# A cross-attention and mixture-of-experts block: where weight reloads and stores stand on a queue, a running sum's engine, the order of background steps, and the ring of gathered rows

## The chip, the core and the metric

The kernel runs on one core of a Trainium2 chip, as one program. The time is in microseconds of the device (us), the median of several runs. One further execution was taken with the hardware profiler; all rows shown come from that one. TensorE (PE) multiplies matrices and PEld is its loading of weights; VectorE (DVE), ScalarE (ACT) and GpSimd (POOL) compute elementwise, and SyncE (SP) and POOL also issue DMA transfers. L12 in a row is line 12 of the kernel before.

## The reference

Two layers on four sequences of 512 tokens with 512 features. First a cross-attention whose probabilities come from a second input and mix the normalized rows, then a block with causal attention (16 heads of 128) and 16 experts, of which each token takes 6, beside a shared expert. Cut to what is computed:

```python
query = features @ Wq.T + bq
key = features @ Wk.T + bk
x = x + softmax(query @ key.T) applied to layernorm(x)

h = rmsnorm(layernorm(x), ln1_w)
q, k, v = h @ wq, h @ wk, h @ wv          # 16 heads of 128
a = softmax(causal(q @ k.T / sqrt(128)))
x1 = layernorm(x) + (a @ v) @ wo
t = rmsnorm(x1, ln2_w)
probs = softmax(t @ gate_w.T)
topv, topi = top_k(probs, 6); topv = topv / sum(topv)
routed = sum over the 6 experts e of topv * down_e(silu(gate_e(t)) * up_e(t))   # inner width 352
shared = sd(silu(sg(t)) * su(t))                                                # inner width 704
out = x + x1 + routed + shared
```

All values are float32 at the interface.

## The kernel before, in words

Every large product is made in three half-precision products: each operand is split into a high and a low f16 part, and `mm3` (L83, L86, L87) issues high by high, high by low and low by high into one bank. `split` makes the two parts, the high one on ACT (L73), the low one on DVE (L74).

**The stages.** `xattn(b)` is a generator: it normalizes batch b's rows, makes the cross-attention, stores the sum to `x_d` and leaves the transposed rows `hT[b]`. `step(b, n)` runs n of its pieces. Batch 0 is run to the end first, batch 1 begins before the heads, and the rest runs in the background of the loop over heads. That loop walks 64 heads (4 batches x 16) in the order of `path`, two heads to a group. For head n it issues `queries` (wqk, one product for query and key), for the first of a group `values` (wv), then `project` of a finished group (wo), `scores` of head n and `attend` of head n - 1 (LAG is 1). When a batch's groups are all projected, `route1`, `route2` and `route3` compute the router, the running place of each token in its expert's list, and the slots. Last in an iteration stand pieces of side work: the residual sums, the `scatter` of routed rows into `xs_d` (96 indirect DMAs on POOL, L467, one per tile of 128 tokens and rank), staging of the shared expert's weights, `pad_rows`, and `step`.

**Weights of the heads.** They are fetched by `fetch` (L406). The first time, a weight is loaded as f32 to a staging tile (L423, on POOL but for wqk1, which SP loads), split into a tile of f16 parts, and that tile is stored to a scratch in DRAM (L429). Later batches reload the f16 tile from there (L414, 40 reloads of 512 KB on POOL's queue). `partner` lets two batches that follow each other in `path` share one fetch. The pools `wp` (wqk) and `wg` (wv, wo) have two buffers for each tag.

**After the heads** come the shared expert of batches 0, 1 and 2 (`gate_up`, `shared_down`), and the 16 experts, ranked by their number of rows. `expert` runs in two halves: `gate_up_rows` makes the inner activation (hf, L1072, is the product of the gate and up branches on DVE, and hT_e, L1058 and L1059, its two f16 parts on ACT and DVE), `down_rows` the output rows yt (L1103 on ACT), which SP stores to `y_d`. Each expert's weights come by SP.

**The gathers.** Beside the last six experts and the last shared expert, the routed rows are gathered back. `gather` (L1169) is an indirect DMA on POOL of 128 rows of 512 f32 (256 KB) into a place of a ring, and `add` (L1178) on DVE multiplies such a tile with the router's weights and adds it to the batch's sum; the adds are held in program order. `lookahead(new, w, keep)` sets the ring: `w` rows share one tile, and `keep` gathers stay ahead of the adds. Before, the tile has three rows and takes turns in the two buffers of tag `hs` in pool `st2`, and four are kept ahead. `tick` spreads the gathers over an expert's steps. At the end of the experts `gather_all(0)` adds all that is left; the last shared expert then uses a ring of three tiles of three rows in pool `xin`, seven kept ahead.

**What sets the order.** The code does not fix it alone: the framework's scheduler places instructions by its own estimate of times and fixes the order on each engine. `pin` holds a few instructions in program order, `after(a, b)` adds an order between two instructions of one queue, without a semaphore. `pace` is a tiny copy on POOL that stands behind the scatters before it and waits for a given value, so that later scatters do not run ahead.

Of the kernel before, what the change touches and what calls it, by code (L numbers as in the profile page):

```python
# [9 lines left out]
F16 = mybir.dt.float16  # L10
F32 = mybir.dt.float32
# [6 lines left out]
P = 128  # L18
# [6 lines left out]
G = 8  # L25
# [14 lines left out]
CW = CAP - CUT  # L40
HB = 64
ON = 60
ROWS = E * T + 1

WS = 256.0
# [10 lines left out]
def xattn_moe_block_kernel(ctx: ExitStack, tc: tile.TileContext, x, xT, ctxT, wqkx, bqk, ln1, ln2,  # L56
# [345 lines left out]
        for j in range(0, 6 * D, 1024):  # L402
            pieces.append((sdw[:, :, j:j + 1024], sd[:, j:j + 1024]))

    held, partner, seen = {}, {}, set()

    def fetch(b, g, pool, tag, n, src, scr, nm):
        if held.get(nm, (None,))[0] == (b, g):
            return held.pop(nm)[1]
        w = pool.tile([P, 2, n], F16, tag=tag, name=f"{nm}_{b}")  # L410
        if (b, g) in partner:
            held[nm] = partner[b, g], w
        if nm in seen:
            nc.gpsimd.dma_start(w.rearrange("p a n -> p (a n)"), scr)  # L414
            return w
        seen.add(nm)
        first = nm in early_st
        if first:
            st_ = early_st[nm]
        else:  # L420
            st_ = stg.tile([P, 1024], F32, tag="st", name=f"{nm}_st")
            q = nc.sync if nm == "wqk1" else nc.gpsimd
            ins = q.dma_start(st_[:, :n], src)  # L423
            if nm == "wqk1":
                after(ins, zz["hT", 0])
        for j, ins in enumerate(split(w[:, 0], w[:, 1], st_[:, :n], WS)):
            if first:
                after(ins, zz["nb"] if j else zz["calm"][0])
        ins = (nc.sync if nm == "wqk0" else nc.gpsimd).dma_start(scr, w.rearrange("p a n -> p (a n)"))  # L429
        if nm != "wqk0":  # L430
            zz["pad"] = ins
        if nm == "wqk0":
            after(ins, zz["ptp", 0])
        return w

    pieces = []

# [17 lines left out]

    def pace(src):
        ins = nc.gpsimd.tensor_copy(mark, src)
        if "rrs" in zz:
            after(ins, zz["rrs"])
        for s in scats:  # L460
            after(ins, s)
        scats[:] = [ins]
# [69 lines left out]
    def route2(b):  # L532
        lg = bank("s", f"lg{b}")
        for t in range(NT):
            tl = slice(t * P, (t + 1) * P)
            n = 0
            for c in range(C):
                for a in range(2):
                    for e in range(2):
                        ins = nc.tensor.matmul(lg[:, t * E:(t + 1) * E], h2T[b][:, a * C + c, tl], gtp[:, e, c, :],  # L540
                                               start=n == 0, stop=n == 15)
                        if b == B - 1 and n == 0:
                            after(ins, zz["gu"])
                        n += 1

        bs = slice(b * NT, (b + 1) * NT)
        lgv = lg[:, :NT * E].rearrange("p (t e) -> p t e", e=E)
        mx = rp.tile([P, NT], F32, name="gmx", bufs=1)
        nc.vector.tensor_reduce(mx, lgv, AX.X, ALU.max)
        pr = rp.tile([P, NT, E], F32, name="gpr", bufs=1)  # L550
        nc.vector.tensor_tensor(pr, lgv, mx.unsqueeze(2).to_broadcast([P, NT, E]), ALU.subtract)
        zz["exp"] = nc.scalar.activation(pr, pr, AF.Exp, scale=PSC)
        sm = rp.tile([P, NT], F32, name="gsm", bufs=1)
        nc.vector.tensor_reduce(sm, pr, AX.X, ALU.add)
        rc = rp.tile([P, NT], F32, name="grc", bufs=1)
        nc.vector.reciprocal(rc, sm)
        nc.vector.tensor_tensor(pr, pr, rc.unsqueeze(2).to_broadcast([P, NT, E]), ALU.mult)
        v8 = rp.tile([P, NT, 8], F32, name="v8", bufs=1)
        i8 = rp.tile([P, NT, 8], U32, name="i8", bufs=1)
        for t in range(NT):  # L560
            nc.vector.max(v8[:, t, :], pr[:, t, :])
            nc.vector.max_index(i8[:, t, :], v8[:, t, :], pr[:, t, :])
        sv = rp.tile([P, NT], F32, name="gsv", bufs=1)
        nc.vector.tensor_reduce(sv, v8[:, :, :K], AX.X, ALU.add)
        rv = rp.tile([P, NT], F32, name="grv", bufs=1)
        nc.vector.reciprocal(rv, sv)
        ix = rp.tile([P, NT, K], F32, name="ix", bufs=1)
        nc.vector.tensor_copy(ix, i8[:, :, :K])
        oh = rp.tile([P, NT * K, E], F32, name="oh", bufs=1)
        nc.vector.tensor_tensor(  # L570
            oh, ix.rearrange("p t k -> p (t k)").unsqueeze(2).to_broadcast([P, NT * K, E]),
            ioe.unsqueeze(1).to_broadcast([P, NT * K, E]), ALU.is_equal)
        mf = rp.tile([P, NT, E], F32, name="mf", bufs=1)
        nc.vector.tensor_reduce(mf, oh.rearrange("p (t k) e -> p t e k", k=K), AX.X, ALU.add)
        mm = rp.tile([P, NT, E], F16, name="mm", bufs=1)
        nc.vector.tensor_copy(mm, mf)
        cs = mf
        for sft in (1, 2, 4, 8):
            nx = rp.tile([P, NT, E], F32, name="rcs", bufs=2)
            nc.vector.tensor_copy(nx[:, :, :sft], cs[:, :, :sft])  # L580
            nc.gpsimd.tensor_tensor(nx[:, :, sft:], cs[:, :, sft:], cs[:, :, :E - sft], ALU.add)
            cs = nx
        nc.gpsimd.tensor_tensor(cs, cs, mf, ALU.mult)
        nc.gpsimd.tensor_tensor(pr, pr, rv.unsqueeze(2).to_broadcast([P, NT, E]), ALU.mult)
        zz[b] = oh, mm, cs, pr
# [36 lines left out]

    def values(b, g):
        hb = hT[b]
        wvt = fetch(b, g, wg, "wv", C * GW, wv[g], wv_d[g], f"wv{g}").rearrange("p a (c d) -> p a c d", c=C)
        vt = vts[b, g] = vp.tile([P, NT, 2, GW], F16, tag="vt", name="vt")
        for t2 in range(0, NT, 2):
            if t2:
                yield
            ps = bank("a", f"v{b}_{g}_{t2}").rearrange("p (t d) -> p t d", t=2)  # L630
            for t in range(t2, t2 + 2):
                tl = slice(t * P, (t + 1) * P)
                mm3(ps[:, t - t2], [(hb[:, c, tl], hb[:, C + c, tl], wvt[:, 0, c], wvt[:, 1, c])
                                    for c in range(C)])
            split(vt[:, t2:t2 + 2, 0], vt[:, t2:t2 + 2, 1], ps, VS * PSC)

    def queries(b, h):
        hb = hT[b]
        wt = fetch(b, h // HG, wp, "wqk", 1024, wqk[h], wqk_d[h], f"wqk{h}").rearrange("p l (a c d) -> p l a c d", a=2, c=C)
        qk = qks[b, h] = []  # L640
        pss = [bank("a", f"qk{b}_{h}_{a}") for a in range(2)]
        w = S // 2 if b == h == 0 else S
        for j in range(0, S, w):
            if j:
                yield
            for a in range(2):
                mm3(pss[a][:, j:j + w], [(wt[:, 0, a, c], wt[:, 1, a, c], hb[:, c, j:j + w], hb[:, C + c, j:j + w])
                                         for c in range(C)])
        for a, ps in enumerate(pss):
            t = hq.tile([P, 2, S], F16, tag=f"qk{a}", name=f"qkt{a}")  # L650
            split(t[:, 0], t[:, 1], ps, PSC * (4.0 / math.sqrt(HD) if a == 0 else 0.25))
            qk.append(t)
# [42 lines left out]
    def project(b, g):  # L695
# [1 line left out]
            x2s[b] = x2p.tile([P, NT, D], F32, tag="x2", name="x2")  # L697
            nc.gpsimd.dma_start(x2s[b], hid_d[b])
        ao, x2 = aos[b, g], x2s[b]
        wot = fetch(b, g, wg, "wo", HG * D, wo[g], wo_d[g], f"wo{g}").rearrange("p a (c d) -> p a c d", c=HG)  # L700
        for t in range(NT):
            tl = slice(t * P, (t + 1) * P)
            ps = bank("w", f"wo{b}_{g}_{t}")
# [76 lines left out]
    for n in range(NH + LAG + 1):  # L780
        if n < NH:
# [13 lines left out]
            for p in parts:  # L795
                for _ in p:
                    pass
        m = n - LAG
        if n == NH:
            last_residual(B - 1)  # L800
# [17 lines left out]
        if 0 <= m < NH:  # L818
            b, h = heads[m]
            attend(b, h)  # L820
            if h % HG == HG - 1:
                ready.append((b, h // HG))
        if n in agenda and n < NH:
            b = agenda[n]
            if n + 1 in agenda:
# [6 lines left out]
        if scat and n < NH:  # L832
            scatter(-(-len(scat) // (min(x for x in ends if x > n) - n + (4 if n > NH - 3 else 0))))
        shared_weights()
        if H // 2 <= n < H // 2 + E:
            pad_rows(n - H // 2)
        if n < 6:
            step(1, 2)
        else:
            for _, j in zip(range(2 - n % 2), bring):  # L840
                step(j)
# [3 lines left out]
    shared_down(0, hs0)  # L845
    cctx.close()
    st2 = ctx.enter_context(tc.tile_pool(name="st2", bufs=2, side="right", reuse_waits="tile"))

    def up(b):
        return gate_up(b, lambda: st2.tile([P, 6 * S], F16, name="hs"), lambda: st2.tile([P, S], F32, name="sgt"))  # L850

    def drip(n, src):
        if scat:
# [340 lines left out]
        for _ in range(-(-len(todo) // left)):  # L1194
            gather()

    lookahead(lambda: st2.tile([P, 3, D], F32, tag="hs", name="yg"), 3, 4)
    ring["steps"] = 1
    for e in range(E):
        wd = nxt  # L1200
        for h, _ in enumerate(expert(wd, e)):
# [4 lines left out]
            if e + 1 < E:  # L1206
# [2 lines left out]
                rows_in(e + 1, h)  # L1209
                if h == 0:  # L1210
                    nxt = ranked_weights(e + 1)
    gather_all(0)
    lookahead(lambda: xin.tile([P, 3, D], F32, tag="xT", name="yg"), 3, 7)
    flush()
    want(K - 1, yrc, cws, y_d)
# [78 lines left out]
```

## Time and profile before

| | |
|---|---|
| runs, us | 1768.77, 1769.27, 1786.13 |
| median, us | 1769.27 |
| the profiled execution, us | 1762.41 |
| its span, us | 1760.7 |
| PE busy | 1708.6 us (97%) |
| DVE busy | 1116.2 us (63%) |
| ACT busy | 829.3 us (47%) |
| POOL busy | 485.1 us (28%) |
| routed rows gathered (L1169) | 96, 109.9 us of POOL |
| routed rows scattered (L467) | 96, 98.7 us of POOL |

The span is what lies between the first and the last instruction in the profile; the execution has 1.7 us around it. The median is 6.9 us above the profiled execution. Busy time of an engine sums its instructions, so an engine at 97% has 52 us in which it does nothing. In the rows of a timeline the columns are the start, the duration, the engine, the line and operation, output and input with shapes, and in brackets the idle time before the instruction and what ended it.

How the span is shared out, in 40 slices of 44 us, each digit the busy share in tenths:

```profile
PE   7899999999998999999999999999999999999998
DVE  6787877787785676776667647544434344356755
POOL 5524212240255242121113454300000000034654
DMA  7787867575687787556547653755554546589866
```

PE is full but for the first slice. POOL is idle while the first ten experts run, and busy again when the gathers begin; there the DMA engines are at their fullest too.

### The profile page before, as it was taken

To read this page: it belongs to the slowest core of one execution; us is meant where nothing else is said; L and a number is where in the kernel's file an instruction comes from. 1 tells how busy PE (TensorE), PEld (TensorE's weight loads), DVE (VectorE), ACT (ScalarE), POOL (GpSimd) and SP (SyncE) were. 2 spreads that over 40 slices of the span, in tenths; PEclk is the share of its full clock that TensorE was granted. 3 is DMA by queue.
4 is the path that set the end of the run, shared out by engine and by line. 5 is a ranking of instruction groups with operands and counts; after the bars stand their busy time and mean duration, and the time that the engine had idled before them with its cause. 6 is when DMAs were issued, how large, how long until landed. Compare 5 with 4: busy or idle time off the path is not lost. (4 is left out here: it accounts for less than half of the span.)

```text
span 1760.7 us, 27659 instructions
## 1 busy us (share of the span) xinstructions
PE 1708.6 (97%) x9919; PEld 932.9 (53%) x9919; DVE 1116.2 (63%) x2766; ACT 829.3 (47%) x1711; POOL 485.1 (28%) x614
## 2 busy tenths in 40 slices
PE   7899999999998999999999999999999999999998
PEld 3555556565654555556555544455555555555553
DVE  6787877787785676776667647544434344356755
ACT  4565655565643545454445422344544445444431
POOL 5524212240255242121113454300000000034654
PEclk9999999999999999999999999999999999999999
DMA  7787867575687787556547653755554546589866
GB/s 246 181 205 184 225 150 192 122 196 118 138 183 187 163 177 179 120 120 118 111 104 132 140 155 128 247 173 148 150 173 137 154 143 163 154 228 254 221 198 213
DMA packets 392212, 296.24 MB, mean 168 GB/s; under 512 B 334880, under 2 KB 335136, under 8 KB 391296
## 3 DMA queue, kind: packets, MB, share of 16 engines
q1 hardware_dynamic: 353360, 159.87, 39.9%
q0 software_dynamic: 38704, 134.51, 25.5%
q8 instruction: 80, 1.31, 0.3%
q14 instruction: 68, 0.56, 0.1%
HBM read 124.81 MB, written 88.94 MB: 121 GB/s over the span
## 5 line engine op out<-in xcount | busy, mean ns | idle before, releaser
L1169 POOL DMA_INDIRECT yg<-y_d,yrc x96 | 109.9, 1145 | 505.2 <-PE u L87 426.0
L673 ACT ACTIVATE pe<-pe,bnm 128x128 f32<-128x128 f32 (+3 forms) x256 | 142.5, 557 | 161.5 <-DVE bnm L671 161.3
L83 PE MATMUL qk<-hT,wqk 128*128 128x512 f16 (+1 forms) x520 | 196.4, 378 | 9.1 <-DMA wqk<-wqk_d 5.5
L86 PE MATMUL qk<-hT,wqk 128*128 128x512 f16 (+1 forms) x520 | 196.5, 378 | 0.0
L87 PE MATMUL qk<-hT,wqk 128*128 128x512 f16 (+1 forms) x520 | 196.3, 377 | 0.0
L74 DVE SCALAR_TENSOR_TENSOR pn<-pe,brc,pn 128x128 f16<-128x128 f32 (+3 forms) x256 | 148.1, 590 | 21.3 <-ACT pn L73 18.0
L671 DVE CUSTOM_DVE_ANT_0 pe<-sc,causal 128x128 f32<-128x128 f32 (+3 forms) x256 | 117.0, 485 | 66.9 <-PE sc L668 65.9
L73 ACT ACTIVATE pn<-pe,brc 128x128 f16<-128x128 f32 (+3 forms) x256 | 133.5, 553 | 34.1 <-ACT pe L673 17.8
L83 PE MATMUL v<-wv,hT 128*128 128x256 f16 x512 | 139.8, 273 | 0.9 <-DMA hT<-hh 0.9
L87 PE MATMUL v<-wv,hT 128*128 128x256 f16 x512 | 139.7, 273 | 0.0
L86 PE MATMUL v<-wv,hT 128*128 128x256 f16 x512 | 139.7, 273 | 0.0
L83 PE MATMUL g<-xT,wt 128*128 128x384 f16 (+2 forms) x384 | 127.3, 331 | 0.0
L86 PE MATMUL g<-xT,wt 128*128 128x384 f16 (+2 forms) x384 | 127.2, 331 | 0.0
L87 PE MATMUL g<-xT,wt 128*128 128x384 f16 (+2 forms) x384 | 127.2, 331 | 0.0
L1058 ACT ACTIVATE hT_e<-hf 128x384 f16<-128x384 f32 (+3 forms) x96 | 51.1, 532 | 133.6 <-DVE hf L1072 133.2
L83 PE MATMUL y<-dt,hT_e 128*128 128x512 f16 (+1 forms) x288 | 109.4, 380 | 0.0
L87 PE MATMUL y<-dt,hT_e 128*128 128x512 f16 (+1 forms) x288 | 108.9, 378 | 0.0
L86 PE MATMUL y<-dt,hT_e 128*128 128x512 f16 (+1 forms) x288 | 108.9, 378 | 0.0
L73 ACT ACTIVATE qkt<-qk 128x512 f16<-128x512 f32 x128 | 75.1, 587 | 70.7 <-PE qk L87 70.5
L705 DVE SCALAR_TENSOR_TENSOR x<-wo,x 128x512 f32<-128x512 f32 x128 | 87.2, 685 | 33.3 <-PE wo L87 32.9
L467 POOL DMA_INDIRECT xs_d<-h2p,slotu x96 | 98.7, 1028 | 28.3 <-issue 27.1
L74 DVE SCALAR_TENSOR_TENSOR qkt<-qk,qkt 128x512 f16<-128x512 f32 x128 | 87.5, 684 | 18.3 <-ACT qkt L73 15.2
(333 smaller groups left out, 4041.5 us busy)
## 6 DMA issues: line engine op xcount, KB each, us to landing
y_d<-yt SPq DMA_DIRECT2D x96, 256.0 KB, 2.8
est<-in_ew_dram SPq DMA_DIRECT2D x32, 704.0 KB, 6.2
est<-in_ed_dram SPq DMA_DIRECT2D x16, 768.0 KB, 4.7
wqk<-wqk_d POOLq DMA_DIRECT2D x20, 512.0 KB, 5.0
wqk_d<-wqk POOLq DMA_DIRECT2D x15, 512.0 KB, 4.0
wqk_st<-in_wqk_dram POOLq DMA_DIRECT2D x14, 512.0 KB, 6.4
xs_d<-causal POOLq DMA_DIRECT2D x16, 384.0 KB, 5.6
wv<-wv_d POOLq DMA_DIRECT2D x10, 512.0 KB, 5.7
```

What stands on the lines that cost most here:

```text
L73: return (nc.scalar.activation(hi, src, AF.Copy, scale=scale), nc.vector.scalar_tensor_tensor(lo, src, scale, hi, ALU.mult, ALU.subtract))
L74: nc.vector.scalar_tensor_tensor(lo, src, scale, hi, ALU.mult, ALU.subtract))
L83: ins = nc.tensor.matmul(o, lh, rh, start=start and j == 0, stop=False)
L86: nc.tensor.matmul(o, lh, rl, start=False, stop=False)
L87: ins = nc.tensor.matmul(o, ll, rh, start=False, stop=stop and j == n - 1)
L467: ins = nc.gpsimd.indirect_dma_start(out=xs_d, out_offset=bass.IndirectOffsetOnAxis(ap=slotu[:, tt, k:k + 1], axis=0), in_=h2ps[tt], in_of ...
L671: nc.vector.tensor_tensor_reduce(pe, ps[:, :w], causal[:, S - w:], -1.0, 3e38, ALU.add, ALU.min, nm)
L673: nc.scalar.activation(pe, pe, AF.Exp, bias=nm, scale=-1.0, accum_out=sm)
L705: nc.vector.scalar_tensor_tensor(x2[:, t, :], ps, 1.0 / (VS * WS), x2[:, t, :], ALU.mult, ALU.add)
L1058: nc.scalar.activation(hT[:R, ic, :w], hf, AF.Copy)
L1169: nc.gpsimd.indirect_dma_start(out=yg, out_offset=None, in_=src, in_offset=bass.IndirectOffsetOnAxis(ap=idx[:, tt, k:k + 1], axis=0))
```

## The change

Six edits.

1. `fetch` gets a flag `early`. With it, a reload is issued and the tile is kept in `soon` until its user asks for it. Heads n + 1's wqk and, where a group begins, wv are asked for right after the queries and values of head n; wo is asked for after `attend` of the group's last head. Weights that have not been staged yet are left to the old place.
2. Stores of staged weights to the scratch are collected in `unsaved`. The next staging load, once issued, is followed by all that wait, in an order on POOL's queue; what is left is issued at the ends of groups.
3. `pace`'s copy is also ordered behind the last reload.
4. The sixteen additions of the routing's running sum (four for each batch) run on DVE, which also makes the copies between them.
5. In the first heads the background of batch 1's cross-attention runs in steps of 3 for heads 1 to 5 (no piece at head 0) where it ran in steps of 2 from head 0.
6. The ring of gathered rows has seven tiles of one row, with five kept ahead, in a pool of its own, which takes the place of the two `hs` tiles. The last shared expert takes its `hs` tiles from the buffers of the experts' weights, so the ring stays open through it; the ring is not drained before the last expert's rows are stored.

```diff
-    held, partner, seen = {}, {}, set()
-
-    def fetch(b, g, pool, tag, n, src, scr, nm):
+    held, partner, seen, soon = {}, {}, set(), {}
+
+    def wqk_of(b, h, early=False):
+        return fetch(b, h // HG, wp, "wqk", 1024, wqk[h], wqk_d[h], f"wqk{h}", early)
+
+    def wv_of(b, g, early=False):
+        return fetch(b, g, wg, "wv", C * GW, wv[g], wv_d[g], f"wv{g}", early)
+
+    def wo_of(b, g, early=False):
+        return fetch(b, g, wg, "wo", HG * D, wo[g], wo_d[g], f"wo{g}", early)
+
+    def fetch(b, g, pool, tag, n, src, scr, nm, early=False):
+        if early and nm not in seen or soon.get(nm) and early:
+            return
         if held.get(nm, (None,))[0] == (b, g):
-            return held.pop(nm)[1]
-        w = pool.tile([P, 2, n], F16, tag=tag, name=f"{nm}_{b}")
+            return None if early else held.pop(nm)[1]
+        w = soon.pop(nm, None)
+        if w is None:
+            w = pool.tile([P, 2, n], F16, tag=tag, name=f"{nm}_{b}")
+            if nm in seen:
+                zz["load"] = nc.gpsimd.dma_start(w.rearrange("p a n -> p (a n)"), scr)
+        if early:
+            soon[nm] = w
+            return
         if (b, g) in partner:
             held[nm] = partner[b, g], w
         if nm in seen:
-            nc.gpsimd.dma_start(w.rearrange("p a n -> p (a n)"), scr)
             return w
         seen.add(nm)
         first = nm in early_st
@@ -423,15 +441,24 @@
             ins = q.dma_start(st_[:, :n], src)
             if nm == "wqk1":
                 after(ins, zz["hT", 0])
+            save(0, None if nm == "wqk1" else ins)
         for j, ins in enumerate(split(w[:, 0], w[:, 1], st_[:, :n], WS)):
             if first:
                 after(ins, zz["nb"] if j else zz["calm"][0])
-        ins = (nc.sync if nm == "wqk0" else nc.gpsimd).dma_start(scr, w.rearrange("p a n -> p (a n)"))
-        if nm != "wqk0":
-            zz["pad"] = ins
         if nm == "wqk0":
-            after(ins, zz["ptp", 0])
+            after(nc.sync.dma_start(scr, w.rearrange("p a n -> p (a n)")), zz["ptp", 0])
+        else:
+            unsaved.append((scr, w))
         return w
+
+    unsaved = []
+
+    def save(keep, behind=None):
+        while len(unsaved) > keep:
+            scr, w = unsaved.pop(0)
+            zz["pad"] = nc.gpsimd.dma_start(scr, w.rearrange("p a n -> p (a n)"))
+            if behind:
+                after(zz["pad"], behind)
...
     def pace(src):
         ins = nc.gpsimd.tensor_copy(mark, src)
-        if "rrs" in zz:
-            after(ins, zz["rrs"])
+        for k in ("rrs", "load"):
+            if k in zz:
+                after(ins, zz[k])
...
-            nc.gpsimd.tensor_tensor(nx[:, :, sft:], cs[:, :, sft:], cs[:, :, :E - sft], ALU.add)
+            nc.vector.tensor_tensor(nx[:, :, sft:], cs[:, :, sft:], cs[:, :, :E - sft], ALU.add)
...
+            if n + 1 < NH:
+                b, h = heads[n + 1]
+                wqk_of(b, h, True)
+                if h % HG == 0:
+                    wv_of(b, h // HG, True)
...
             if h % HG == HG - 1:
                 ready.append((b, h // HG))
+                wo_of(b, h // HG, True)
...
+        if n % HG == HG - 1:
+            save(1)
+        if n >= 3 * G:
+            save(0)
...
         if n < 6:
-            step(1, 2)
+            step(1, 3 * (n > 0))
...
+    hctx = ctx.enter_context(ExitStack())
+    hsp = hctx.enter_context(tc.tile_pool(name="hsp", bufs=2, side="right", reuse_waits="tile"))
 
     def up(b):
-        return gate_up(b, lambda: st2.tile([P, 6 * S], F16, name="hs"), lambda: st2.tile([P, S], F32, name="sgt"))
+        return gate_up(b, lambda: (hsp.tile([P, 6 * S], F16, name="hs") if b < B - 1 else
+                                   mw.tile([P, IP * 4], F32, tag="est", name="hs", bufs=3).bitcast(F16)),
+                       lambda: st2.tile([P, S], F32, name="sgt"))
...
-    lookahead(lambda: st2.tile([P, 3, D], F32, tag="hs", name="yg"), 3, 4)
+    hctx.close()
+    ring_p = ctx.enter_context(tc.tile_pool(name="ring", bufs=RING, side="right", reuse_waits="tile"))
+    lookahead(lambda: ring_p.tile([P, 1, D], F32, name="yg"), 1, RING - 2)
...
-    gather_all(0)
+    gather_all()
     lookahead(lambda: xin.tile([P, 3, D], F32, tag="xT", name="yg"), 3, 7)
```

The uses of `fetch` in `queries`, `values` and `project` become `wqk_of`, `wv_of` and `wo_of`; `RING` is 7.

More of the change, by code (lines that the diff above doesn't have):

```diff
@@ L42 @@
 ON = 60
+RING = 7
 ROWS = E * T + 1
@@ L624, in values @@
         hb = hT[b]
-        wvt = fetch(b, g, wg, "wv", C * GW, wv[g], wv_d[g], f"wv{g}").rearrange("p a (c d) -> p a c d", c=C)
+        wvt = wv_of(b, g).rearrange("p a (c d) -> p a c d", c=C)
         vt = vts[b, g] = vp.tile([P, NT, 2, GW], F16, tag="vt", name="vt")
@@ L638, in queries @@
         hb = hT[b]
-        wt = fetch(b, h // HG, wp, "wqk", 1024, wqk[h], wqk_d[h], f"wqk{h}").rearrange("p l (a c d) -> p l a c d", a=2, c=C)
+        wt = wqk_of(b, h).rearrange("p l (a c d) -> p l a c d", a=2, c=C)
         qk = qks[b, h] = []
@@ L699, in project @@
         ao, x2 = aos[b, g], x2s[b]
-        wot = fetch(b, g, wg, "wo", HG * D, wo[g], wo_d[g], f"wo{g}").rearrange("p a (c d) -> p a c d", c=HG)
+        wot = wo_of(b, g).rearrange("p a (c d) -> p a c d", c=HG)
         for t in range(NT):
```

## The prediction, before the change was run

> **What bounds the kernel now.** I read the page's engine totals first, then TensorE's waits, then those waits by stretch of the span, then the timeline around the longest ones. TensorE is busy 1708.6 of 1760.7 us (97%), so everything in this change plays for the 52.1 us in which it is not busy, plus what a long pause costs afterwards in clock. TensorE's waits (columns: total us, times, longest):
>
> ```profile
> PE av L83 <- DMA pt<-pn: 16.9, 10, 3.9
> PE xm L83 <- DMA ptp<-pn: 9.8, 2, 5.8
> PE qk L83 <- DMA wqk<-wqk_d: 5.5, 1, 5.5
> PE u L1081 <- DVE hf L1072: 3.9, 2, 2.1
> PE qk L83 <- DMA hT<-hh: 3.6, 2, 3.2
> ```
>
> The largest row, the flipped probabilities (pt), is touched by no edit. A weight reload is waited for once, the ranked experts' end twice. By stretch (length, then busy time and instructions of PE, PEld, DVE, ACT, POOL; PE clock; DMA share; GB/s):
>
> ```profile
> 88.00:540.00 452.00, 446.32 (x2742) 254.97 (x2740) 354.50 (x986) 254.94 (x570) 134.32 (x183) 1.00 0.72 172
> 540.00:1016.00 476.00, 458.45 (x2879) 263.85 (x2878) 323.32 (x938) 234.30 (x556) 136.88 (x207) 0.99 0.64 140
> 1016.00:1544.00 528.00, 527.98 (x2831) 269.34 (x2830) 241.10 (x476) 219.86 (x371) 58.45 (x81) 1.00 0.55 160
> 1544.00:1650.00 106.00, 102.08 (x573) 55.85 (x572) 66.41 (x101) 44.61 (x79) 48.76 (x43) 1.00 0.91 239
> ```
>
> Idle: 5.7 us in the first heads, 17.5 in the later ones, nothing in 1016-1544, 3.9 where gathers run beside experts, 17.2 before 88 us and about 8 after 1650. The timeline at the places that the edits touch:
>
> ```profile
> 76.60 0.58 PE L83 MATMUL xm<-ptp,lnp 128*128 128x512 f16 x1 [3.97 <-DMA ptp<-pn]
> 138.86 0.38 PE L83 MATMUL qk<-hT,wqk 128*128 128x512 f16 x1 [0.39 <-DMA hT<-hh]
> ...
> 538.93 0.96 POOL L467 DMA_INDIRECT xs_d<-h2p,slotu  x1 [0.30 <-issue]
> 539.89 0.60 POOL L414 DMA_DIRECT2D wqk<-wqk_d  x1
> 548.81 0.61 PE L83 MATMUL qk<-hT,wqk 128*128 128x512 f16 x1 [5.51 <-DMA wqk<-wqk_d]
> ...
> 1615.89 1.22 POOL L1169 DMA_INDIRECT yg<-y_d,yrc  x1 [4.15 <-DVE acc L1178]
> 1620.09 1.43 DVE L1178 SCALAR_TENSOR_TENSOR acc<-yg,cws,acc 128x512 f32<-128x512 f32 x2 [3.81 <-DMA yg<-y_d,yrc]
> 1621.57 0.60 ACT L1103 ACTIVATE yt<-y 128x512 f32<-128x512 f32 x1 [6.72 <-DMA y_d<-yt]
> 1626.41 0.32 PE L1081 MATMUL u<-xT,wb 128*128 128x384 f16 x1 [2.13 <-DVE hf L1072]
> ```
>
> The reload is issued 8.9 us before TensorE goes on and stands behind ten scatters of about 1.28 us each on POOL (525.7 to 539.9); TensorE came for it at 543.3.
>
> **Part 1, reloads ahead.** The change issues a reload at the end of the queries or values before. I compared the two programs' order on POOL: all 40 reloads stand where they stood, but for one (head 1's wqk ahead of wo, where TensorE waited for neither), and each waits for the same matmul to free its buffer. The framework's scheduler already issued them as early as the two buffers allow. The one that TensorE waits for is still behind the same ten scatters. Its buffer was free at about 534.9, when qk of the head before was done; only a place ahead of the last four scatters would gain. So the 5.5 us stay: 0. Bounds: a gain of 5.5 plus about 2.5 for 549-553, where the granted clock is 0.50 (8 in all), if the timing of these ten scatters slips behind it; a loss of a scatter step, 1.3.
>
> **Part 2, stores behind loads.** 31 stores of weights (0.56 us of issue each) move behind the next staging load on POOL, one or two places. Nothing is added. Store and load take the same queue; the next writer of the same weight buffer, two fetches later, waits longer. ACT's share of the splits already waits 26.1 us in 15 places for these stores, and behind it stand exponentials. Yet TensorE waits for no split weight at all, because the splits end before it comes for them (a head lasts 1016 / 64 = 15.9 us): that hides it, 0. Without that cover each of the 15 would cost TensorE its mean, 1.7 us. The added order of the mark behind the load is on one queue: no semaphore, 0.
>
> **Part 3, running sum.** POOL loses 12 x 269 ns + 4 x 294 = 4.4 us. DVE has no such row; the nearest, a 128x64 tensor-tensor, takes 0.19 to 0.22, so 16 x 0.2 = 3.2 us are added. The waits of DVE for POOL's sum (4.1 us in 3) go. The ten scatters start when the rank matmul is done (520.1) and DVE's rb (520.4), not on these. On no path of TensorE: 0, bounds -1.6 (the scatters' start moves by the longest of these waits) to +1.
>
> **Part 4, the next batch's cross-attention in steps of 3 for heads 1-4.** This does reorder TensorE: the first third differs from 72 us to 540, the rest is the same but for two or three rows. At 72.4 TensorE took the flip's matmul and waited 3.97 us; then some ten matmuls at half rate (0.427 against 0.2155 us apart, about 1.5-2 us lost). In the new order two score matmuls come first, waiting for DVE reads at 75.34 and 75.95: 2.98 + 0.3 us. Gain 4.0 - 3.3 = 0.7. Whether the half clock goes with it is weighed here. The Trainium skill ("TensorE: Matmul & The Clock Gate", section "HAM oscillation — how this bites in real kernels") has TensorE throttled by idle windows of about 3.4 us; by it 2.98 would escape, and the gain would be about 2.2. In this trace 3.23 us of idle at 51.3 already halved the rate, and 2.48 at 585 did not. 2.98 lies between, nearer to 3.23; the row decides, I take 0.7 and keep 2.2. hT of batch 1 is made a head earlier, which ends 138.86's wait: -0.4. What is late next: the exponentials and pt flips of heads 1-5 meet a denser cross-attention. Bounds: the first heads' 4.8 us of pt waits gone, or the later heads' density (12 us in 476) over 452: 11.4, 6.6 more. No row prefers either: 0.
>
> **Part 5, the gather ring.** Six rows as two tiles of three become seven single rows. Before, the first gather of a tile waits for an add issued just before it; now for one that stands two gathers back. POOL's 45.1 us of waiting for adds (16 times) mostly goes, but POOL binds nothing here. Two TensorE pauses end in this stretch. At 1645.26 (1.80 us) hf stood on DVE behind an add whose gather had waited 6.5 us for its tile: gone, -1.8. At 1626.41 (2.13) ACT's yt waited for a store of y_d, under a full DMA load (share 0.91): I take half, -1.0. No drain at the ring's end: adds move on, DVE is 66 of 106 us busy, 0.
>
> A rule that speaks against a gain is "DMA: Bandwidth & Descriptors", section "Anatomy of one DMA — SWDGE (gpsimd) path": about 2.0 us plus bytes over 436 GB/s, so 2.6 us for a gather of 256 KiB. By that, four adds of lookahead (4 x 0.745 = 3.0 us of DVE) cover every gather and the ring is worth nothing, and 548.81's load (512 KiB, 3.2 us) would have landed at 543.1, before TensorE came. The rows say otherwise:
>
> ```profile
> L1169 POOL DMA_INDIRECT yg<-y_d,yrc x96: 953/960/2612, 1551.4 to 1739.6; - x96
> DMA to landing us min/median/max: 3.3/4.7/10.6
> ```
>
> so the row is taken. By the rule the sum is -1.1, by the rows: -0.7 - 0.4 - 1.8 - 1.0 = -3.9.
>
> **Sum.** The profiled run took 1762.41 (span 1760.7 and 1.7 around it): 1762.4 - 3.9 = 1758.5. The median of the runs, 1769.27, is 6.9 above it; against that: 1765.4, so 1765.
>
> **Rivals.** *Faster by more than the sum.* The reload's stall and its half clock vanish (8), part 4 gives 2.2 and the early pt waits 4.8, the ring all 3.9, hT 0.4: 19.3, so 1750. For it: slots are free 5 us before that reload goes out. Against: POOL's order, which is fixed, puts the ten scatters ahead.
>
> *Slower, by the ring.* Five gathered rows now wait ahead of the adds and up to seven gathers fly, where DMA is at 0.91 already. A gather's packets then delay y_d's stores; yt waits for these (28.7 us in 9 waits of ACT after 1540), hT behind yt on ACT, and TensorE takes a pause as at 1626.41. Price: about 2 us for each of the ten half experts, 20 in all: 1789. It decides when the y_d stores regularly land over 7.6 us, as before that pause; their median is 3.6 after 1540. For it: two pauses of this form stand there already. Against: the number of rows moved is the same, and TensorE paused twice in 106 us.
>
> *The change does not do what it says.* The reloads come no earlier, the ring was never on the path, and the reordered heads trade one wait for another: 0 to +8, so 1769 to 1777.
>
> **How the numbers follow.** Forecast 0.54; no effect or a small loss 0.22; faster rival 0.10; slower rival 0.14. One per cent, about what a measurement of this kernel can tell, is 17.7 us: faster means under 1751.6, slower over 1787.0. Only the two rivals reach beyond: faster 0.10, same 0.76, slower 0.14. The range leaves out the faster rival's far half and most of the slower one: from 1752 (the reload's 8, the ring, 2.2, hT and half of the pt gain, 17) to 1780 (6.6 of pt, 1.3 of scatter, 3 more of ring).
>
> **What would show it.** Right: 5 to 6 us of wait for wqk<-wqk_d near 545 behind ten scatters; 2.9 us at the first scores near 75; no pause behind hf near 1640, POOL's waits for acc well under 45. Wrong: a wait list for pt far from 17 us; the reload issued well before TensorE needs it; y_d's stores landing over 7 us and new pauses at L1081. The forecast fails if the head stretch up to 540 moves by more than 7 us either way.

## The result, and the profile after

| | before | after |
|---|---|---|
| median, us | 1769.11 (21 runs) | 1787.38 (21 runs) |
| range, us | 1754.3 to 1786.13 | 1773.52 to 1798.73 |
| the profiled execution, us | 1762.41 | 1776.03 |
| its span, us; granted clock | 1760.7; 0.993 | 1774.2; 0.991 |

The ratio is 1.0114, with a 95% interval of 1.009 to 1.0137: the change costs some 20 us, where 4 us less were forecast, and the median lies 7 us above the range. The profiled execution is the second fastest of its 21 runs, so its 13.5 us of longer span show the loss too small. The run at the median, 1787.38, has a span of 1785.7 and a granted clock of 0.986 where the profiled one has 0.991; 0.014 x 1785.7 against 0.009 x 1774.2 is 25 against 16 us, so by this estimate up to 9 of the 11 us between the two spans lie in the clock. In rows of other kernels than the one before, the line numbers are those of that kernel.

TensorE's waits in the changed kernel (total us, times, longest):

```profile
PE av L84 <- DMA pt<-pn: 19.5, 11, 6.1
PE qk L84 <- DMA hT<-hh: 7.1, 2, 3.9
PE xm L84 <- DMA ptp<-pn: 6.0, 1, 6.0
PE u L1123 <- DVE hf L1114: 4.4, 2, 3.0
PE xixp L1020 <- DVE xixd L1018: 2.8, 1, 2.8
PE sc L695 <- DVE qkt L75: 2.7, 1, 2.7
PE qk L84 <- DMA wqk<-wqk_d: 2.5, 1, 2.5
```

The flip of the cross-attention's probabilities (ptp) is waited for 3.8 us less, the reload (wqk) 3.0 less. Against this stand the transposed rows hT with 3.5 more, pt with 2.6 more, and two new rows, xixp and qkt. The sums hide where it happens. By stretch (columns as before):

```profile
88.00:540.00 452.00, 433.55 (x2638) 245.90 (x2637) 344.72 (x957) 242.81 (x542) 125.95 (x168) 0.99 0.70 165
540.00:1016.00 476.00, 465.86 (x2942) 269.44 (x2940) 331.13 (x968) 239.67 (x569) 141.81 (x207) 0.99 0.64 143
1544.00:1650.00 106.00, 101.64 (x563) 55.19 (x562) 64.00 (x97) 45.03 (x79) 48.06 (x39) 0.98 0.94 231
```

TensorE is idle for 18.4 us in the first heads where it was for 5.7, for 10.1 in the later ones where it was for 17.5, and for 4.4 beside the gathers where it was for 3.9. The same product found in both traces, and how much later it starts after the change:

| product | before, us | after, us | lag, us |
|---|---|---|---|
| qk, the 193rd | 157.6 | 160.2 | 2.6 |
| qk, the 577th | 392.5 | 404.4 | 11.9 |
| qk, the 769th | 517.9 | 529.7 | 11.8 |
| qk, the 1057th | 699.1 | 702.9 | 3.8 |
| g, the first of the experts | 1134.0 | 1140.2 | 6.2 |
| g, the 1057th | 1656.3 | 1664.4 | 8.1 |
| the end | 1760.7 | 1774.2 | 13.5 |

The first heads lose 11.9 us, against the 7 that the prediction named as its point of failure; the waits for pt and the reload between 518 and 700 give 8 back in this execution, and the rest comes after 1000: xixp's 2.8 us near 1114, some 2 us more beside the gathers, and some 3 us in five pauses of the last shared expert, near 1735 to 1741, that wait for nothing that the profile shows. The cause of these was not tried. Two pauses stand at the start of the loss; the timeline of the changed kernel has

```profile
142.24 0.38 PE L84 MATMUL qk<-hT,wqk 128*128 128x512 f16 x1 [3.85 <-DMA hT<-hh]
180.77 0.61 PE L84 MATMUL av<-pt,vt 128*128 128x512 f16 x1 [6.11 <-DMA pt<-pn]
```

The first is the wait that the prediction saw vanish (0.39 us at 138.86 before). What happened around it is in the issues of two transfers: the last flip of batch 1's hT (a DMA transpose on SP's queue, DMA_TRANSPOSE) and the 1 MB load of batch 2's x. Before:

```profile
135.76 1.26 SPq L91 DMA_TRANSPOSE hT<-hh  x1
136.59 0.84 POOL L215 DMA_DIRECT2D xt<-in_x_dram  x1 [0.30 <-POOL x L354]
```

After, with the other transfers of POOL at this place:

```profile
127.88 0.54 POOL L459 DMA_DIRECT2D wo_d<-wo  x1
131.05 0.85 POOL L216 DMA_DIRECT2D xt<-in_x_dram  x1 [0.30 <-POOL x L355]
131.81 2.60 SPq L92 DMA_TRANSPOSE hT<-hh  x1
134.46 0.54 POOL L441 DMA_DIRECT2D wqk_st<-in_wqk_dram  x1 [2.56 <-DVE wo L75]
134.99 0.54 POOL L459 DMA_DIRECT2D wo_d<-wo  x1
```

Before, the flip goes out 0.83 us ahead of the load and is used 3.1 us later. After, it goes out 0.76 us behind the load and is used 10.4 us later.

### The profile page after: what moved, and what is told of

Its sections match the earlier page's. It is cut to its first block, busy times and chain, and to the rows that moved or that the text cites. A ratio compares the mean times of both kernels' runs of the same rounds, so it can differ in the third digit from the quotient of the medians.

```text
span 1774.2 us, 27650 instructions
## 1 busy us (share of the span) xinstructions
PE 1714.3 (97%) x9919; PEld 933.1 (53%) x9919; DVE 1120.1 (63%) x2782; ACT 827.9 (47%) x1711; POOL 492.4 (28%) x598
## 5 line engine op out<-in xcount | busy, mean ns | idle before, releaser
L1211 POOL DMA_INDIRECT yg<-y_d,yrc x96 | 118.0, 1229 | 505.0 <-DVE hf L1114 434.6
L495 POOL DMA_INDIRECT xs_d<-h2p,slotu x96 | 98.8, 1030 | 28.0 <-issue 26.8
```

The costliest lines, as they stand in the source:

```text
L495: ins = nc.gpsimd.indirect_dma_start(out=xs_d, out_offset=bass.IndirectOffsetOnAxis(ap=slotu[:, tt, k:k + 1], axis=0), in_=h2ps[tt], in_of ...
L1211: nc.gpsimd.indirect_dma_start(out=yg, out_offset=None, in_=src, in_offset=bass.IndirectOffsetOnAxis(ap=idx[:, tt, k:k + 1], axis=0))
```

## The experiments

Each ratio is against the kernel before on the same chip, with its 95% interval. The chips differ between the groups of runs, so across groups it is the ratios that are compared, not the times.

**The heads, the ring, the steps, the stores, each by itself** (e1 to e4). e1 has all edits but the running sum and the ring; e2 has the ring alone, the diff of which stands above.

```diff
+            step(1, 3 * (n > 0))                        # e3, alone
...
+            save(0, None if nm == "wqk1" else ins)      # e4, alone, with save at the group ends
```

> The kernel before with the edits to the heads alone: early reloads, stores behind loads, the mark behind the load, steps of 3; the running sum on POOL and the old ring. Theory A (the reordered first heads cost it: waits for hT near 142 and for pt near 181, with half a clock after each): 1.007 to 1.012 of before, +12 to +21 us, and a profile with waits of 3 us or more for hT and pt between 100 and 200 us. Theory B (the ring costs it): 0.998 to 1.003. If both share it: 1.004 to 1.007.

> The kernel before with the ring of seven rows alone, everything ahead of 1500 us in the order of before. Theory B (the gathers take DMA time from the stores of y_d and from code loading in the last shared expert): 1.004 to 1.011, +7 to +20 us, all of it after 1540, with pauses behind hf of 2 to 3 us and waits in sg and su near the end. Theory A: 0.997 to 1.002. My prediction's own step had -2.8 us here, 0.998.

> The kernel before with the steps of 3 alone. Theory A1 (the denser cross-attention of batch 1 is what makes hT and pt late): 1.005 to 1.012. Theory A2 (the stores behind the loads are): 0.997 to 1.003. My prediction had -1 us.

> The kernel before with the stores of weights behind the next staging load alone. Theory A2 (the later store holds the weight buffer, so the next split is late and with it the exponentials that stand behind it on ACT): 1.005 to 1.012. Theory A1: 0.997 to 1.003. My prediction had 0.

| run | median, us | ratio |
|---|---|---|
| e1, heads | 1787.42 | 1.0096 (1.0057 to 1.0135) |
| e2, ring | 1773.48 | 1.001 (0.9987 to 1.0033) |
| e3, steps of 3 | 1765.32 | 0.9975 (0.9954 to 0.9995) |
| e4, stores | 1782.23 | 1.0075 (1.0042 to 1.0109) |

The loss is in the heads, and in the stores: the edit that the prediction had priced at nothing. The ring is worth nothing that these runs can tell, the steps gain a little. In e4 the wait for hT is the longest of its trace:

```profile
142.89 0.84 POOL L216 DMA_DIRECT2D xt<-in_x_dram  x1 [0.30 <-DMA wo_st<-in_wo_dram]
143.16 1.25 SPq L92 DMA_TRANSPOSE hT<-hh  x1
157.09 0.59 PE L84 MATMUL qk<-hT,wqk 128*128 128x512 f16 x1 [11.77 <-DMA hT<-hh]
```

Here too the load is ahead, by 0.27 us. Theory A2 came with a mechanism, the store that keeps its buffer and so holds up the next split. The traces do not show it: in the lists of ACT's waits of the changed kernel and of e4 no store of a weight appears, only the staging loads. (That of e1 names one store, 3.1 us, but of a wv, ahead of a split that writes a wqk.) The other half of the theory, exponentials that stand behind a late split, comes back below.

**Each suspect taken out of the changed kernel** (e5 to e8). e5 puts the stores back, e6 delays the pads, e7 delays batch 2's cross-attention and its load, e8 does all three.

```diff
+            save(0)                             # e5, e8: right behind unsaved.append
...
-        if H // 2 <= n < H // 2 + E:
-            pad_rows(n - H // 2)
+        if H <= n < H + E:                      # e6, e8
+            pad_rows(n - H)
...
-        else:
+        elif n >= 9:                            # e7, e8
             for _, j in zip(range(2 - n % 2), bring):
```

> The changed kernel with one edit undone: each weight is stored to its scratch where it was before, right after its split is issued. If the stores behind the loads are the whole loss: 0.995 to 1.001 of before (the steps of 3 alone gave 0.9975, the ring 1.001), and no wait of 5 us for pt between 170 and 200 us. If the rest of the change has a loss of its own beside it: 1.003 or more.

> The changed kernel with the sixteen pad transfers (384 KB each, which stand behind the stores on POOL's queue) eight heads later; the stores stay behind the loads, and POOL's order is the same up to the first pad near 157 us. Theory traffic (a flip of pt is out while a staging load, a store and two pads run at once, and its small packets and theirs slow each other): the wait for pt near 181 falls from 6.1 to under 3, the time by 4 to 8 us to 1.006 to 1.009. Theory hold (the store keeps the weight's buffer, so the next split and the exponentials behind it are late): nothing changes, 1.010 to 1.013. Neither touches the wait for hT near 142.

> The changed kernel with batch 2's cross-attention begun three heads later, so that its 1 MB load of x and its loads of xT and ctx no longer run beside the flips of batch 1's hT. Theory traffic: the wait for hT near 142 (3.9 to 11.8 us in the profiles with moved stores) falls under 2 and the time by 3 to 8 us, to 1.006 to 1.010. Theory hold: no change, 1.010 to 1.013. The heads from 9 on get the later pieces, so a pt wait there may grow by 1 to 3 us.

> The changed kernel with the stores where they were before, the pads eight heads later and batch 2's cross-attention three heads later: a try for a version that beats both. Theory traffic: 0.990 to 0.997, with no wait over 2 us for hT or pt between 100 and 200 us. Theory hold: 0.997 to 1.000.

| run | median, us | ratio |
|---|---|---|
| e5, stores back | 1773.1 | 1.0032 (1.0006 to 1.0057) |
| e6, late pads | 1792.41 | 1.0147 (1.0116 to 1.0179) |
| e7, late x | 1779.63 | 1.0087 (1.0056 to 1.0119) |
| e8, all three | 1781.21 | 1.0084 (1.0052 to 1.0115) |

e5 takes 0.8 of the 1.1% away and keeps a small loss, as its second branch had it. The other three missed. In e6 the wait near 181 fell to about 3 us (3.05, at 184) as the traffic theory had it, but there are new waits for pt (4.76 us at 421, 5.60 at 610), and the time rose. That the pads cause them is not shown: they now go out between 246 and 575 us, the last one 35 us ahead of the second wait. In e7 the scheduler moved the load with the flip: it now goes out 0.04 us behind it, and the wait is 7.10 us. e8 has no wait for batch 1's hT and still loses it later (5.96 us for pt at 306, 4.56 at 423); by what was not tried.

What these runs did give is a series. Over the traces so far in which TensorE waits for this flip (e8 is the one left out), how far the load of x stands behind the flip of hT (negative: ahead of it), and the time from the flip's issue to the product that waits for it:

| run | load behind flip, us | flip to use, us |
|---|---|---|
| before | 0.83 | 3.1 |
| e2 | 0.82 | 3.1 |
| e3 | 0.40 | 7.7 |
| e5 | 0.39 | 6.7 |
| e7 | 0.04 | 9.7 |
| e4 | -0.27 | 13.9 |
| after | -0.76 | 10.4 |
| e6 | -0.87 | 15.4 |
| e1 | -1.05 | 14.2 |

Nothing in the program orders the two: the flip waits for ACT and DVE, the load for POOL's last use of batch 1's tile. It is a race, decided by about a microsecond. Each row is one execution, and their spread is wide: up to this place the changed kernel and e6 run the same instructions in the same order, and have 10.4 and 15.4 us.

**The race decided by hand** (e9 to e12). The load of batch 2's x goes to SP's queue, on which the flips are, and is ordered there behind the last flip of hT (e9, e11, e12) or ahead of it (e10). e9 is the changed kernel, e10 the one before, e11 has the steps of 3, e12 the stores.

```diff
-        feed(b).dma_start(xt, x[b].rearrange("(t p) d -> p t d", p=P))
+        ins = (nc.sync if b == 2 else feed(b)).dma_start(xt, x[b].rearrange("(t p) d -> p t d", p=P))
+        if b == 2:
+            after(ins, zz["hT", 1])             # e10: after(zz["hT", 1], ins)
```

> The changed kernel with one transfer moved: the 1 MB load of batch 2's x goes out on SP's queue right behind the last flip of batch 1's hT, not on POOL's, where it now starts 0.76 us ahead of that flip. Theory race (the flip is late when the load goes out ahead of it or with it: 3 us from issue to use at 0.8 us behind in the kernel before, 7 to 15 us at 0.4 behind to 1.05 ahead in six others): the wait for hT near 142 is under 1 us and the time falls by 5 to 12 us, to 1.004 to 1.009 of before; the wait for pt near 181 stays. Theory order (the new order of the engines makes hT itself late): the wait stays above 3 us, 1.010 to 1.013.

> The kernel before with the same load ahead of that flip on SP's queue, no weight store moved. Theory race: a wait of 5 to 12 us for hT near 145 with half a clock after it, 1.003 to 1.009 of before. Theory order or hold: 0.998 to 1.002.

> The kernel before with the steps of 3 and the load behind the flip: a try for a version that beats both. Theory race: the 4.8 us wait for hT of the steps alone (0.9975) goes with its half clock, 0.992 to 0.997. Otherwise 0.997 to 1.000.

> The kernel before with the stores behind the loads (1.0075 alone) and the load of x behind the flip. If the stores cost mainly through this race: the wait of 11.8 us for hT near 157 goes, 0.998 to 1.003. If they cost mainly at the pt waits near 105 and 195 or elsewhere: 1.004 to 1.008.

| run | median, us | ratio |
|---|---|---|
| e9, after, load behind | 1776.8 | 1.0028 (1.0004 to 1.0053) |
| e10, before, load ahead | 1772.31 | 1.0023 (1.0001 to 1.0045) |
| e11, steps of 3, load behind | 1757.81 | 0.9949 (0.9929 to 0.9968) |
| e12, stores, load behind | 1774.5 | 1.0041 (1.0021 to 1.0061) |

In e9 TensorE does not wait for batch 1's hT at all, and one transfer moved takes 0.86% off, three quarters of the loss. The load ahead costs the kernel before 0.2%, less than expected: the flip takes 6.9 us from issue to use, with a wait of 3.13 us and no half clock after it (granted clock 1.00 from 145 to 152). Both e9 and e10 have the load on SP's queue, so the queue by itself is not what gains. In e12 the wait near 141 is 1.28 us, and the stores still cost 0.4%, the second branch of its expectation. e11 beats both kernels, 0.5% (some 9 us) below before.

Four kernels now stand with and without the load behind the flip (e13 is shown below): the changed one gains 0.86%, e3 to e11 0.26%, e4 to e12 0.34%, e5 to e13 0.49%. All four gain, but only the intervals of the first pair lie apart. A rival is that the edit lets the scheduler rearrange everything else too. It does not: between the traces of e3 and e11 and of e5 and e13 the order of instructions on every engine is the same but for the load itself, between e4 and e12 but for two of DVE's, and in e9 24 of TensorE's products and a few instructions of DVE and ACT change places around the flip. What stays open is the size: in e9's profiled execution, the second slowest of its 15 runs, the 169th qk starts 6.4 us sooner than in the changed kernel's (135.8 for 142.2), the 577th only 0.6 (403.8 for 404.4).

e11's trace shows a second thing: with the steps of 3 and the stores in their old place, the scheduler puts the reload ahead of the ten scatters (in e3, e5 and e13 too).

```profile
529.41 0.60 POOL L428 DMA_DIRECT2D wqk<-wqk_d  x1
532.09 1.14 POOL L497 DMA_INDIRECT xs_d<-h2p,slotu  x1 [0.19 <-issue]
533.53 1.00 POOL L497 DMA_INDIRECT xs_d<-h2p,slotu  x1 [0.30 <-issue]
```

The wait for it, 5.5 us before and 2.5 after, is gone from e11's list of TensorE's waits:

```profile
PE av L84 <- DMA pt<-pn: 11.5, 8, 3.6
PE xm L84 <- DMA ptp<-pn: 6.0, 1, 6.0
PE qk L84 <- DMA hT<-hh: 4.7, 2, 3.2
PE sc L696 <- DVE bnm L701: 2.8, 1, 2.8
PE u L1110 <- DVE hf L1101: 2.4, 1, 2.4
```

So the reload can come ahead. The early issue of edit 1 is not what does it (e3 and e11 do not have it), and the changed kernel, with its stores behind the loads, does not have the reload there.

**What is left** (e13 to e15). With the race decided, e13 takes the stores out of the changed kernel, e15 the ring; e14 is the kernel before with the running sum on DVE alone.

> The changed kernel with the stores where they were and the load of x behind the flip of hT: all edits but one, and the race decided. If the stores hold the rest of the loss (a wait of 6.5 us for the probabilities near 178, and the reload near 560 still behind ten scatters): 0.993 to 0.998, with neither of the two waits. If the ring or the sum holds it: 1.000 to 1.004.

> The kernel before with the running sum on DVE alone. My prediction had 0 and bounds of -1.6 to +1 us: 0.998 to 1.002. If the sum's place on DVE holds up exponentials: 1.003 or more, with new waits of TensorE for pt near 515 and 710.

> The changed kernel with the load of x behind the flip and the old ring of two tiles of three rows (1.0028 with the new one). If the ring is worth nothing either way, as alone (1.001): 1.000 to 1.005. If it costs beside the other edits: below 1.000. If it gains, as I predicted: above 1.004.

| run | median, us | ratio |
|---|---|---|
| e13, no stores, load behind | 1762.2 | 0.9983 (0.9955 to 1.0011) |
| e14, running sum | 1764.14 | 1.001 (0.9976 to 1.0043) |
| e15, no ring, load behind | 1771.39 | 1.0039 (1.0013 to 1.0065) |

The stores hold the rest too: 1.0028 with them, 0.9983 without, though the two intervals just overlap. The runs that have them moved and the race decided (e9, e12, e15) show one wait of 5.8 to 6.5 us that e13 does not have; in e9's trace it is

```profile
178.34 0.59 PE L84 MATMUL av<-pt,vt 128*128 128x512 f16 x1 [6.53 <-DVE pn L75]
```

The order on ACT shows why these probabilities are late. In e9 their first exponentials (pe) stand behind the split of a wqk, which waits for its staging load, though DVE had their input ready at 170:

```profile
169.91 0.08 DVE L701 DVE_READ_ACCUMULATOR2_ANT bnm<- 128x1 f32 x1
172.13 1.06 ACT L74 ACTIVATE wqk<-wqk_st 128x1024 f16<-128x1024 f32 x1 [3.41 <-DMA wqk_st<-in_wqk_dram]
173.57 0.39 ACT L703 ACTIVATE pe<-pe,bnm 128x128 f32<-128x128 f32 x1
```

In e13, the same kernel with the stores in their old place, they stand ahead of it:

```profile
169.48 0.40 ACT L703 ACTIVATE pe<-pe,bnm 128x128 f32<-128x128 f32 x1 [1.90 <-DVE bnm L701]
172.95 1.06 ACT L74 ACTIVATE wqk<-wqk_st 128x1024 f16<-128x1024 f32 x1 [2.98 <-DMA wqk_st<-in_wqk_dram]
```

ACT waits for the load in both; what changed is who stands behind it. The order is the scheduler's answer to the moved stores. In every trace with the stores moved and batch 2's cross-attention not delayed (after, e1, e4, e6, e9, e12, e15) the split stands ahead of these exponentials, and TensorE waits 3.05 to 7.6 us for the probabilities between 178 and 196 us. In every one with the stores in their old place (before, e2, e3, e5, e10, e11, e13, e14) it stands behind, and no such wait is over 2.7 us.

The reload tells less. e9 and e12 wait for it 7.5 and 8.2 us where the changed kernel and e4 waited 2.5 and 0.2, in the same order on POOL, but the kernel before waits 5.5, e10 8.6 and e14 9.8 for it, with no store moved. From issue to use it took 5.5 to 13.9 us in the traces that have it behind the ten scatters. Part of what e12 wins at hT is lost again there: its 169th qk starts 16.1 us sooner than e4's, its 1057th 7.4. And e13 has a wait of 7.9 us for pt near 593 instead.

Edits 1 and 3 were not run alone. Between e11 (0.9949) and e13 (0.9983) they come in together with the sum and the ring; the difference is 0.34%, and the intervals overlap.

## Why the prediction was wrong, point by point

- **Stores behind loads, 0.** This is the step that failed: "That hides it, 0". The reason was that TensorE waits for no split weight. The line before it had named what does wait, the exponentials behind the splits on ACT, and they were not followed on to TensorE, nor was it asked what a moved transfer does to other transfers. The runs show both in its place: the scheduler put a split ahead of exponentials (3.05 to 7.6 us of wait near 180), and the flip of hT lost its race against the load of x (waits of 3.85 to 11.8 us between 142 and 157 us where the stores are moved and the race is not decided). The stores alone cost 0.75%, and 0.82% in the changed kernel (1.0114 against 1.0032 without them); with the race decided about 0.4% is left. The 26.1 us that the text gave as ACT's waits for stores in 15 places were, in the list of ACT's waits, waits for the staging loads, in 14.
- **Steps of 3, -1.1.** Right in sign, by themselves: 0.9975. But the term for hT, -0.4, was a loss: hT is flipped earlier, TensorE comes for it earlier, and in the changed kernel the flip is behind the 1 MB load. The wait grew from 0.39 to 3.85 us, and to 4.82 in e3, where no store is moved. The first difference at 72 us went as worked out or better: the wait of 3.97 us is gone, and no 2.98 us took its place in this execution (in e3's there are 3.06, and the granted clock is 0.57 from 76 to 80, so the half clock stays, as the 0.7 had it).
- **The cover of the first heads.** "No row prefers either: 0." For the steps alone the runs bear this out (0.9975). But the first heads of the whole change lost 11.9 us, beyond the bound of 6.6: it was made from pt waits of a denser cross-attention only, not from hT and not from the stores.
- **Reloads a step ahead, 0.** Right for the changed kernel as to the place: the reload is still behind ten scatters, issued at 551.11 and waited for until 557.67. The wait is 2.46 us and not 5.5 mainly because the load took 6.6 us from issue to use where it took 8.9, which no edit aimed at. That the scheduler could not place it better was wrong, as e11 shows.
- **Running sum, 0.** 1.001, within its interval of 0.
- **Ring, -2.8.** Not borne out. Alone it is 1.001, and taken out it makes 1.0039 of 1.0028. POOL's waits for adds, which were to go mostly, went from 45.1 to 39.2 us only:

```profile
POOL yg L1211 <- DVE acc L1220: 39.2, 15, 7.2
```

DVE's waits for gathered rows did fall, from 26.8 to 12.1 us, but TensorE's two pauses behind hf are still there, 4.4 us for 3.9.
- **The rivals.** The one on the slower side had the right result by the wrong mechanism: it put contention of transfers at the gathers, where the ring alone cost nothing clear of its interval (1.001), and not at the flips of the first heads. The one by which the change does not do what it says held for the reload and the ring.

## What to carry to other kernels

When a transfer is moved on a queue, look not only for who waits for it, but for which small, urgent transfer is issued within a few microseconds of its new place on any queue. Where a flip and a large load are free to go out in either order, give them one: a single ordered load took back three quarters of what six edits had cost here, and 0.26 to 0.49% in three other kernels. Where a scheduler sets the order, look also at what it puts behind an instruction that waits for a load: the same wait of ACT cost TensorE little or some 6 us by whether exponentials stood behind it. And compare an edit alone and in company: the steps of 3 gain 0.25% by themselves, and beside the moved stores that gain does not show (e4 1.0075, e1 1.0096).

## What was not expected of the hardware

A flip that goes out beside a large transfer lands late: 7 to 15 us from issue to use in the series above, against 3. In the DMA view of the kernel before, from 128 to 132 us, the flips are nearly by themselves (packets, MB, share of the time of 16 engines):

```profile
q1 hardware_dynamic: 1697, 0.43, 56.7%
```

In the same view from 140 to 144 us the large packets are:

```profile
q0 software_dynamic: 304, 1.18, 89.8%
```

And in e4, while TensorE waits for hT, from 150 to 154 us, both run:

```profile
DMA packets 409, 0.31 MB, mean 78 GB/s; under 512 B 353, under 2 KB 353, under 8 KB 409
...
q0 software_dynamic: 59, 0.23, 87.6%
q1 hardware_dynamic: 350, 0.08, 26.7%
```

By count and share, a large packet took 0.898 x 16 x 4 us / 304 = 0.19 us by itself and 0.876 x 64 / 59 = 0.95 us in these 4 us, a flip's packet 21 and 49 ns. But these are the worst 4 us of that wait. Just before them, from 146 to 150 us, both run as well, and a large packet took 0.756 x 64 / 242 = 0.20 us:

```profile
q0 software_dynamic: 242, 0.93, 75.6%
q1 hardware_dynamic: 715, 0.18, 31.8%
```

The shares add up to over 100% because the times of packets overlap, so they do not show that the engines were full. Over the whole wait, from 143 to 157.2 us, e4 moved much the same per us as the kernel before did from 136 to 148 with the same three large transfers:

```profile
DMA packets 3428, 3.05 MB, mean 215 GB/s; under 512 B 2851, under 2 KB 2851, under 8 KB 3428
DMA packets 2726, 2.64 MB, mean 220 GB/s; under 512 B 2212, under 2 KB 2212, under 8 KB 2724
```

So in e4 what suffers in the mixture is the small transfer that is waited for, not the sum. By what rule the engines choose between the two was not measured.

And one pause is not one price: the runs of one program spread over 25 us, and their granted clock goes with the time on the whole, from 0.989 at 1773.5 to 0.982 at 1798.7 us. Which of the two causes the other was not tried.
